# Last image of a state-space, attention and expert-layer kernel: where its first-choice rows are gathered, where its bias is added, and where its residual is kept

## The chip, the cores and the metric

The kernel runs on one core of a Trainium2 chip. Its time is the device time of one execution in microseconds. Shown for the kernel before are three timed runs and one profiled execution; a trace of the profiled execution gives every instruction of every engine. The engines are TensorE (PE, with its weight loads PEld), VectorE (DVE), ScalarE (ACT), GpSimd (POOL) and SyncE, whose queue SP issues nearly all DMAs. All data are fp32.

## The reference, cut to what matters

Four images of 384 channels by 1024 positions pass through three layers. Only the last one, and the sum behind it, is touched here:

```python
# layer 0: four-direction selective scan, normalised, GELU, added to x
# layer 1: t = t + attention(layernorm(t))            # t: (1024 tokens, 384) per image
t = t + ffn(layernorm(t))                             # t on the right is the residual

def ffn(x):                                           # 4 experts, 2 chosen per token
    probs = softmax(x @ gate_w + gate_b)
    masked = probs kept at the two largest, divided by their sum   # the two shares
    h = gelu(einsum("bsd,edh->ebsh", x, w1) + b1[:, None, None, :])      # hidden 1536
    y = einsum("ebsh,ehd->ebsd", h, w2) + b2[:, None, None, :]
    return einsum("bse,ebsd->bsd", masked, y)
```

So the output of one token is its residual, plus share times row of its first expert, plus share times row of its second, where each row has had that expert's bias b2 added.

## The kernel before, in words

The program is written out in "ticks" by generators: each tick lets the scan, the attention, the expert layer and a list of side jobs (`side`) issue a few instructions, and every engine then works through its own instructions in that order. Images 0 to 2 have their attention and expert layer laid beside the scan of the next image. The last image has nothing beside it (`alone`, b = 3), and the end of the program is its expert layer and a closing sum.

**Routing.** `chosen` (L1390) works on groups of 4, 2 and 2 tiles of 128 tokens. It finds the two experts of each token and a place for each of its two rows: expert e owns the rows from e*1024 on of a DRAM array `xs_d`, and the rows of one expert are packed. In `places`, column 0 is the smaller row number, so the first choice is always the lower-numbered of the two experts; column 1 is the second choice. `scatter` (L1513) writes token rows to `xs_d` by 16 indirect DMAs from POOL. The gates (shares by expert) are transposed by PE (L1538), copied by ACT (L1543) and stored to `gates_d` (L1559). `table` (L1565) works out the expert and the block number of each of NBLK = 11 blocks of 256 rows, clipped at L1596 to the 16 blocks that the array has, and how many rows of each block are filled (0, up to 128, up to 256).

**Expert layer.** `experts` (L1622) walks the blocks in the order "1" 0, "1" 1, "2" 0, "1" 2, "2" 1, ... , "1" 10, "2" 9, "2" 10, where "1" is the product with w1 and GELU, "2" the product with w2. PE runs `first_` (L1758) and `second_` (L1808) under branches that skip empty halves of a block; a wholly empty block gets only small fill transposes (L1766, L1817). The weights come in chunks of 384 KB into 8 shared SBUF slots by L1664 on the SP queue. When "2" of block j is done, `out_` (L1824) copies its two halves of 128 rows to the tile `yt`, one half by ACT (L1829), one by DVE (L1827), and `kept` (L1836) stores the tile to the DRAM array `ys_d` (L1837), also on SP. ACT does its copy behind the GELUs of the next block's "1" that stand ahead of it, and what SP holds behind a store (the next chunks of w2) waits for that store.

**Closing sum of the last image.** `kept` of block 2 starts `beside_all` (L1947): for each of the 8 token tiles a load of the residual t2 from DRAM into `z` (L1955; it was stored there by attention at L1266), a load of the gates (L1956), and an ACT scaling of an identity by the second share (L1958). `kept` of block 9 starts `first_choice` (L2021): POOL gathers the first-choice rows of the 8 tiles out of `ys_d` (L1880) and DVE adds share times row to `z` (L1967). `kept` of block 10 starts `late` (L2030): POOL gathers the second-choice rows; PE sums `z` by identity (L1977) and the bias as b2 times gates (L1980) for all 8 tiles, then adds the second choice (L2041), ACT copies the sum (L1913) and SP stores it (L1914).

**What orders these.** A tile is tracked as a whole. A gather from `ys_d` waits for every store to it that stands ahead in the program, and a store to it waits for every gather that stands ahead. A PSUM tile that is two banks wide (`y_end`, `v_end`) is tracked as one, so a reader of one bank can wait for work on the other. [...]

Of the kernel before, what the change touches and what calls it, by code (L numbers as in the profile page):

```python
# [54 lines left out]
CAP = L  # L55
NBLK = 2 * L // BT + E - 1


@with_exitstack
def hybrid_kernel(  # L60
# [146 lines left out]
    gates_d = [dram.tile([E, L], F32, tag=f"gt_{b}", name=f"gtd_{b}") for b in range(B)]  # L207
    xs_d = [dram.tile([E * CAP, C], F32, tag=f"xs_{i}", name=f"xsd_{i}") for i in range(1)]
    ys_d = [dram.tile([E * CAP, C], F32, tag=f"ys_{i}", name=f"ysd_{i}") for i in range(1)]
    views = dram_disjoint_views(xs_d[0], 2 * L // P)  # L210
    g_d = dram.tile([P, M, C], F32, tag="g", name="g_d")
    wv_d = dram.tile([P, M, C], F32, tag="wv", name="wv_d")
# [116 lines left out]
    def later():  # L329
        yield "wait", 8  # L330
        for t, src in (
            (dsk, d_skip), (lnw, ln_w), (lnb, ln_b),
            (gw, gate_w.rearrange("(c p) e -> p c e", p=P)), (gb, gate_b.partition_broadcast(P)),
        ):
            nc.sync.dma_start(t, src)
            yield "wait", 1
        yield "wait", 2
        nc.vector.tensor_reduce(dsum, dsk, AX.X, ALU.add)
        yield "wait", 40
        zero = yield from slots.take("zero", P, C)  # L340
        nc.gpsimd.memset(zero, 0.0)
        yield "wait", 2
        for t in (*xs_d, *ys_d):
            for o in range(0, E * CAP, 8 * P):
                nc.sync.dma_start(
                    t[o : o + 8 * P, :].rearrange("(r p) d -> p r d", p=P),
                    zero.unsqueeze(1).to_broadcast([P, 8, C]),
                )
                yield "wait", 6
        slots.give("zero")  # L350
        for m in range(M):
            nc.sync.dma_start(b2s[:, m * P : (m + 1) * P], b2[:, :, m].rearrange("p e -> e p"))
            yield "wait", 4


# [762 lines left out]
    def attention(b, yb, fx0):  # L1118
# [117 lines left out]
        def values(i):  # L1236
# [14 lines left out]
            def rows():  # L1251
# [17 lines left out]

                if alone:  # L1270
                    kept()
                else:
                    defer(2, kept)
# [116 lines left out]
    def chosen(b, h, sc, rows):  # L1390
# [142 lines left out]
        mts = []  # L1533
        for part in parts:
            pm = yield from banks.take(f"pm_{name}_{part[0]}")
            for q in part:
                o = (q - part[0]) * P
                nc.tensor.transpose(pm[:E, o : o + P], mk[:, q, :], ident)  # L1538
            yield "pe", 0.12 * len(part)
            mt = yield from slots.take(f"mt_{name}_{part[0]}", E, 512)  # L1540
            mts.append(mt)
            yield "wait", 1
            nc.scalar.copy(mt[:, : len(part) * P], pm[:E, : len(part) * P])  # L1543
            banks.give(f"pm_{name}_{part[0]}")
# [20 lines left out]
    def table(b, total):  # L1565
# [29 lines left out]
        nc.vector.tensor_tensor(which[:, 1, :], which[:, 1, :], turn_of[:, :, 0], ALU.add)  # L1595
        nc.vector.tensor_scalar_min(which[:, 1, :], which[:, 1, :], float(E * CAP // BT - 1))  # L1596
        nc.vector.tensor_copy(n, total)
# [24 lines left out]
    def experts(b, route):  # L1622
# [6 lines left out]
        chunks = [(w, j, c) for w, j in order_ for c in range(6)]  # L1629
        tiles, biases = {}, {}  # L1630
        fetched = [0]
        expert, block = {}, {}

        def look_up(j):
            if j == 0:
                expert[j] = block[j] = 0
            if j not in expert:
# [4 lines left out]
                    tables[b][0:1, NBLK + j : NBLK + j + 1], min_val=0,  # L1642
                    max_val=E * CAP // BT - 1,
                )

        def weights():
# [4 lines left out]
            if w == "1":  # L1651
# [140 lines left out]
        def second_(j, gone):  # L1792
# [31 lines left out]
            def out_():  # L1824
                for i in range(2):
                    if alone and i == 1 and j < NBLK - 1:
                        nc.vector.tensor_copy(yt[:, i, :], pss[i][:, :C])  # L1827
                    else:
                        nc.scalar.copy(yt[:, i, :], pss[i][:, :C])  # L1829
                    banks.give(f"py_{b}_{j}_{i}")  # L1830
# [5 lines left out]
            def kept():  # L1836
                nc.sync.dma_start(rows_of(ys_d[0], j), yt)  # L1837
# [39 lines left out]

    def gather(b, i, g, k):

        nc.gpsimd.indirect_dma_start(  # L1880
            out=g[:, k * C : (k + 1) * C], out_offset=None, in_=ys_d[0],
            in_offset=bass.IndirectOffsetOnAxis(ap=places[b][:, i, k : k + 1], axis=0),
        )
# [27 lines left out]
    def put_out(b, i, ps, z):  # L1911

        nc.scalar.copy(z[:, C : 2 * C], ps[:, :C])  # L1913
        nc.sync.dma_start(  # L1914
            out[b, :, i * P : (i + 1) * P].rearrange("(m p) l -> p m l", p=P),
            z[:, C : 2 * C].rearrange("p (m t) -> p m t", m=M),
        )
# [29 lines left out]
    def beside_all(b):  # L1947

        for i in range(L // P):
            g = dtp.tile([P, L], F32, tag=("dt4", "du4")[i // 4], name=f"g_{b}_{i}")  # L1950
            z = (hp if i < 7 else dap).tile(
                [P, L], F32, tag="h" if i < 7 else "da", name=f"z_{b}_{i}"
# [3 lines left out]
            nc.sync.dma_start(g[:E, 2 * C : 2 * C + P], gates_d[b][:, bass.ts(i, P)])  # L1956
            for k in range(2) if b < B - 1 else (1,):
                act(  # L1958
# [4 lines left out]

    def add_choice(b, i, k):

        g, z = closing[b, i]
        nc.vector.scalar_tensor_tensor(  # L1967
            z[:, :C], g[:, k * C : (k + 1) * C], shares[b][:, i, k : k + 1], z[:, :C],
            ALU.mult, ALU.add,
        )  # L1970

    def sum_up(b, i, ps, last):

        g, z = closing[b, i]
        for m in range(M):
            s = bass.ts(m, P)
            nc.tensor.matmul(ps[:, s], z[:, s], ident, start=(m == 0), stop=False)  # L1977
        for m in range(M):
            s = bass.ts(m, P)
            nc.tensor.matmul(  # L1980
                ps[:, s], b2s[:, s], g[:E, 2 * C : 2 * C + P], start=False,
                stop=(last and m == M - 1),
            )
# [36 lines left out]

    def first_choice(b):  # L2021

        for i in range(L // P):
            gather(b, i, closing[b, i][0], 0)
        yield "wait", 2
        for i in range(L // P):
            add_choice(b, i, 0)
            yield "wait", 0

    def late(b):  # L2030
# [4 lines left out]
        for i in range(L // P):  # L2035
            pss[i] = yield from banks.take(f"pz_{b}_{i}")
            sum_up(b, i, pss[i], False)
        for i in range(L // P):
            g, z = closing[b, i]
            for m in range(M):  # L2040
                nc.tensor.matmul(  # L2041
                    pss[i][:, bass.ts(m, P)], g[:, C + m * P : C + (m + 1) * P],
                    z[:, 2 * C + P : 2 * C + 2 * P], start=False, stop=(m == M - 1),
                )
# [181 lines left out]
```

## Time and profile before

| | |
|---|---|
| timed runs | 3621.86, 3630.05, 3631.2 us; median 3630.05 |
| profiled execution | 3634.82 us; span of its trace 3633.1 us; mean granted TensorE clock 0.856 |
| PE busy / DVE busy / ACT / POOL | 80% / 80% / 58% / 55% of the span |
| scan of the four images | first to last scan row, 50.1 to 3054.7 us of the span |
| normalisation, attention and routing of the last image | about 3055 to 3270 us |
| its expert layer | about 3270 to 3588 us |
| its closing sum | about 3588 to 3633 us |
| DMA of the program | 799.22 MB, 220 GB/s on average |

A row of the timeline gives start and length in microseconds, engine, source line, operation, output and inputs, and in brackets how long the engine had been idle and what released it. Matmuls of fp32 show two records each. Instructions that only issue a DMA stand on the queue's own rows (SPq). The clock column of the windows is the granted TensorE clock as a share of full speed. The engines' shares are averages over stages; the last 550 us, in which the scan is over, are read by themselves.

### The profile page before, as it was taken

The numbers are of one execution on the slowest core, as the hardware profiler recorded it, in microseconds if no ns is written. First come the engines' busy times: TensorE is split into PE (matmuls) and PEld (weight loads), VectorE is DVE, ScalarE is ACT, GpSimd is POOL, SyncE is SP. The second block draws the span as 40 slices with busy tenths as digits, with TensorE's granted clock in tenths as the row PEclk, the third lists the DMA queues.
The fourth block names the chain that finished last, engine by engine and source line by source line (L and its number), as shares of the span: only waits on it lengthen the run. The fifth ranks groups of instructions, "written<-read, shape, count | busy, mean of one in ns | idle before, by whom it ended". The sixth has DMA issues, their size and how long they took to land.

```text
span 3633.1 us, 42851 instructions
## 1 busy us (share of the span) xinstructions
PE 2902.2 (80%) x12982; PEld 1682.8 (46%) x12982; DVE 2898.7 (80%) x2148; ACT 2090.0 (58%) x3375; POOL 1982.5 (55%) x950
## 2 busy tenths in 40 slices
PE   4666676778599999679589996678499985889998
PEld 1333333334255664345246562344166651557776
DVE  6998888998999999989998999999999997130000
ACT  4888888557477666458466665457265663332121
POOL 2777677645666566855665556856766666010001
PEclk7777876789699999789689998789599997979997
DMA  6677665554579987644578887644488884125665
GB/s 189 225 257 266 231 220 187 198 171 169 193 250 331 319 307 280 219 176 155 174 251 300 288 309 270 208 161 150 161 297 279 313 309 142 44 75 166 201 198 160
DMA packets 405252, 799.22 MB, mean 220 GB/s; under 512 B 47500, under 2 KB 278620, under 8 KB 404972
## 3 DMA queue, kind: packets, MB, share of 16 engines
q1 hardware_dynamic: 390572, 770.01, 61.3%
q0 software_dynamic: 8192, 25.17, 2.1%
q8 instruction: 165, 2.70, 0.3%
q10 hardware_dynamic: 6208, 0.39, 0.1%
q14 instruction: 115, 0.94, 0.1%
HBM read 680.44 MB, written 115.02 MB: 219 GB/s over the span
## 4 chain that ended last, share of the span: by engine, by line
PE 31%; DVE 27%; DMA 4%; issue 2%; ACT 2%; SPq 0%; POOL 0%; DVEq 0%; ACTq 0%; POOLq 0%
DVE h L716 14%; DVE v L710 9%; PE ph L1758 8%; PE py L1808 7%; PE y L758 2%; DMA w<-in_w 2%; PE v_end L1808 2%; PE y_end L1808 1%; PE pq L1144 1%; PE pv L1155 1%; PE y_end L1758 1%; PE v_end L1758 1%; ACT ht L196 1%; PE ss L1174 0%; PE pdt L566 0%
## 5 line engine op out<-in xcount | busy, mean ns | idle before, releaser
L733 POOL TENSOR_TENSOR h<-h,bc 128x1024 f32<-128x1024 f32 x768 | 1816.8, 2369 | 1101.2 <-DVE v L710 881.3
L716 DVE TENSOR_TENSOR_SCAN h<-da,v 128x1024 f32<-128x1024 f32 x768 | 1749.9, 2284 | 75.6 <-PE v L1032 38.3
L196 ACT ACTIVATE da<-dt,a 128x1024 f32<-128x1024 f32 x768 | 882.5, 1159 | 712.9 <-DVE h L716 587.7
L710 DVE TENSOR_TENSOR v<-du,bc 128x1024 f32<-128x1024 f32 x664 | 863.3, 1300 | 80.3 <-PE y L758 35.4
L758 PE MATMUL y<-h,sel 128*32 128x512 f32 x3072 | 629.3, 719 | 266.6 <-POOL h L733 250.3
L1758 PE MATMUL ph<-turned,w 128*128 128x256 f32 (+1 forms) x2568 | 534.8, 363 | 15.0 <-DMA w<-in_w 9.3
L1808 PE MATMUL py<-w,ht 128*128 128x384 f32 x1416 | 485.9, 493 | 19.0 <-DMA w<-in_w 19.0
L1758 PEld LDWEIGHTS ph<-turned,w 128*128 128x128 f32 x2568 | 449.2, 192 | 105.1 <-issue 17.0
L758 PEld LDWEIGHTS y<-h,sel 128*32 128x32 f32 x3072 | 110.3, 121 | 656.3 <-POOL h L733 416.5
L1808 PEld LDWEIGHTS py<-w,ht 128*128 128x128 f32 x1416 | 265.6, 191 | 233.5 <-issue 46.1
L196 ACT ACTIVATE ht<-ph,b1t 128x256 f32<-128x256 f32 x470 | 195.7, 472 | 238.7 <-PE ph L1758 211.6
L1880 POOL DMA_INDIRECT g<-ysd,places x64 | 85.7, 1338 | 345.8 <-DMA ysd<-yt 329.9
L196 ACT ACTIVATE st<-turn,bt 128x128 f32<-128x128 f32 x832 | 242.6, 543 | 0.0
L1032 PE MATMUL v<-ident,st 128*128 128x128 f32 x832 | 149.1, 339 | 100.0 <-DVE h L716 92.1
L1032 PEld LDWEIGHTS v<-ident,st 128*128 128x128 f32 x832 | 122.3, 176 | 147.1 <-DVE h L716 88.8
L186 ACT ACT_TABLE_LOAD x122 | 156.5, 1283 | 13.2 <-issue 11.0
L566 PE MATMUL pdt<-xd,wdt 12*128 12x512 f32 x184 | 108.9, 739 | 23.8 <-ACT st L196 13.5
L1515 POOL DMA_INDIRECT xsd<-fx,places x32 | 38.7, 1209 | 142.4 <-issue 138.9
L1827 DVE COPY yt<-y_end 128x384 f32<-128x384 f32 x3 | 1.7, 558 | 128.1 <-ACT ht L196 60.1
L1245 PE MATMUL po<-vt,pt 128*128 128x384 f32 x234 | 86.6, 518 | 6.2 <-ACT pt L1135 6.2
L196 ACT ACTIVATE ht<-ht 128x3072 f32<-128x3072 f32 x33 | 91.2, 2765 | 0.4
L1174 PE MATMUL ss<-axn,qt 128*128 128x512 f32 (+3 forms) x240 | 87.1, 503 | 2.8 <-ACT pr L196 1.7
(433 smaller groups left out, 2748.4 us busy)
## 6 DMA issues: line engine op xcount, KB each, us to landing
w<-in_w SPq DMA_DIRECT2D x528, 384.0 KB
bc<-rows SPq DMA_DIRECT2D x384, 512.0 KB
dt<-dts SPq DMA_DIRECT2D x192, 512.0 KB
du<-dts SPq DMA_DIRECT2D x192, 512.0 KB
dts<-dt SPq DMA_DIRECT2D x48, 512.0 KB
dts<-du SPq DMA_DIRECT2D x48, 512.0 KB
xg<-xsd SPq DMA_DIRECT2D x44, 384.0 KB
ysd<-yt SPq DMA_DIRECT2D x44, 384.0 KB
```

The lines of the kernel that those rows point to most:

```text
L186: nc.scalar.preload_act_table_set(kind)
L196: return nc.scalar.activation(dst, src, f, **more)
L566: nc.tensor.matmul(pss[i], wdt[r, m * P : (m + 1) * P], xd[r, bass.ts(h, 512)], start=True, stop=True,)
L710: return nc.vector.tensor_tensor(u["v"], spread["du4", n], spread["bc", n][:, 0, :], ALU.mult)
L716: nc.vector.tensor_tensor_scan(u["h"][:, ::step], u["da"][:, ::step], u["v"][:, ::step], 0.0, op0=ALU.mult, op1=ALU.add,)
L733: product = units[n]["product"] = nc.gpsimd.tensor_tensor(h, h, spread["bc", n][:, 1, :], ALU.mult)
L758: units[n]["row"] = nc.tensor.matmul(y, sel, h, start=first, stop=last, tile_position=(0, jj * DJ))
L1032: nc.tensor.transpose(u["v"][:, t * P : (t + 1) * P], st[:, t, u["j"] * P : (u["j"] + 1) * P], ident)
L1174: nc.tensor.matmul(ps[:, : e - o], qt[:, c, i * P : (i + 1) * P], xn[o // 512][:, c, : e - o], start=(c == 0), stop=(c == M - 1 and (alone ...
L1245: nc.tensor.matmul(po[:, :C], pts[i][:, j, :], vt[:, j, :], start=False, stop=(j == i))
L1758: nc.tensor.matmul(ps[:, i * BT : i * BT + n], t[:, c, i * P : (i + 1) * P], xt[:, c, :n], start=(c == 0), stop=(c == M - 1),)
L1808: nc.tensor.matmul(pss[i][:, :C], hts[j][:, 2 * c + f, i * P : (i + 1) * P], tiles["2", j, c][0][:, f, :], start=(c == 0 and f == 0), stop ...
```

## The change

1. `ys_d` and `xs_d` grow from 4096 to ROWS = 4864 rows, so that empty surplus blocks get rows of their own, and the clip in `table` goes. The zero fill of both at the start (`later`) grows from 8 to 10 DMAs. `ys_d` gets two views that are declared disjoint: `up_to_last` and `the_last`. In the last image, blocks 0 to 9 are stored through the first, block 10 through the second.
2. First choices are gathered through `up_to_last`, at one of two places, by branches that POOL takes. Behind block 8, if block 9 belongs to the last expert (no first choice is of the last expert, so all their rows are then stored); else behind block 9. The additions of share times row stand behind block 9 as before.
3. b2 is also written to DRAM once (`b2_d`); for each block of the last image its expert's row is loaded to all 128 partitions (`b2t`), on SP's queue ahead of the block's first w2 chunk. Both halves of `yt` are made by DVE as PSUM plus `b2t`; ACT makes none.
4. The residual stays in SBUF (`yb`): its stores, its loads, the gates' transposes, copies, stores and loads of the last image go; DVE adds the first choice into `yb`; the closing PE sum is `yb` by identity and the second choice, without the bias product; `late` uses the gather tile for its copy.

On the engines' order up to the routing of the last image, only SP's rows change (more zero fill, the write of `b2_d`, later b2 loads), and three clips on DVE go. In DVE's order at the end stand: two additions of block 9, eight first-choice additions, two additions of block 10.

```diff
+ROWS = E * CAP + (NBLK - 2 * L // BT) * BT
-    ys_d = [dram.tile([E * CAP, C], F32, tag=f"ys_{i}", name=f"ysd_{i}") for i in range(1)]
+    ys_d = [dram.tile([ROWS, C], F32, tag=f"ys_{i}", name=f"ysd_{i}") for i in range(1)]
+    b2_d = dram.tile([E, C], F32, tag="b2", name="b2_d")
+    up_to_last, the_last = dram_disjoint_views(ys_d[0], 2)
...
-            for o in range(0, E * CAP, 8 * P):
+            for o in range(0, ROWS, 8 * P):
+                n = min(8, (ROWS - o) // P)
...
+        nc.sync.dma_start(b2_d, b2s)
...
-                if alone:
-                    kept()
-                else:
+                if not alone:
                     defer(2, kept)
...
-        for part in parts:
+        for part in () if alone else parts:
...
+                if alone and c == 0:
+                    b2ts[j] = bcp.tile([P, 2, L], F32, tag="bc", name=f"b2t_{b}_{j}")[:, 0, :C]
+                    row_ = b2_d[bass.ds(e, 1), :]
+                    nc.sync.dma_start(
+                        b2ts[j], bass.AP(
+                            tensor=row_.tensor, offset=row_.offset, ap=[[0, P], row_.ap[-1]]
+                        )
+                    )
...
-                    if alone and i == 1 and j < NBLK - 1:
-                        nc.vector.tensor_copy(yt[:, i, :], pss[i][:, :C])
+                    if alone:
+                        nc.vector.tensor_tensor(yt[:, i, :], pss[i][:, :C], b2ts[j], ALU.add)
...
-                nc.sync.dma_start(rows_of(ys_d[0], j), yt)
+                there = (up_to_last if j < NBLK - 1 else the_last) if alone else ys_d[0]
+                nc.sync.dma_start(rows_of(there, j), yt)
...
+                elif alone and j == NBLK - 3:
+                    side.append(first_choice(b, True))
                 elif alone and j == NBLK - 2:
                     side.append(first_choice(b))
...
     def beside_all(b):
...
+            if b == B - 1:
+                closing[b, i] = g, g[:, :C]
+                act(g[:, 2 * C : 2 * C + P], ident, AF.Copy, scale=shares[b][:, i, 1:2])
+                yield "wait", 1
+                continue
...
+    def add_choice(b, i):
+
+        g, _ = closing[b, i]
+        t2 = ybs[b][:, :, bass.ts(i, P)]
         nc.vector.scalar_tensor_tensor(
-            z[:, :C], g[:, k * C : (k + 1) * C], shares[b][:, i, k : k + 1], z[:, :C],
+            t2, g[:, :C].rearrange("p (m t) -> p m t", m=M), shares[b][:, i, 0:1], t2,
             ALU.mult, ALU.add,
         )
...
-    def first_choice(b):
+    ahead_of = {}
 
-        for i in range(L // P):
-            gather(b, i, closing[b, i][0], 0)
+    def first_choice(b, soon=False):
+
+        def gathers():
+            for i in range(L // P):
+                gather(b, i, closing[b, i][0], 0, up_to_last)
+
+        if soon:
+            ahead_of[b] = nc.gpsimd.value_load(
+                tables[b][0:1, NBLK - 2 : NBLK - 1], min_val=0, max_val=E - 1
+            )
+            with tc.If(ahead_of[b] > E - 2):
+                gathers()
+            return
+        with tc.If(ahead_of[b] < E - 1):
+            gathers()
         yield "wait", 2
         for i in range(L // P):
-            add_choice(b, i, 0)
+            add_choice(b, i)
             yield "wait", 0
```

More of the change, by code (lines that the diff above doesn't have):

```diff
@@ L207, in hybrid_kernel @@
     gates_d = [dram.tile([E, L], F32, tag=f"gt_{b}", name=f"gtd_{b}") for b in range(B)]
-    xs_d = [dram.tile([E * CAP, C], F32, tag=f"xs_{i}", name=f"xsd_{i}") for i in range(1)]
-    ys_d = [dram.tile([E * CAP, C], F32, tag=f"ys_{i}", name=f"ysd_{i}") for i in range(1)]
+    xs_d = [dram.tile([ROWS, C], F32, tag=f"xs_{i}", name=f"xsd_{i}") for i in range(1)]
+    ys_d = [dram.tile([ROWS, C], F32, tag=f"ys_{i}", name=f"ysd_{i}") for i in range(1)]
     views = dram_disjoint_views(xs_d[0], 2 * L // P)
+    b2_d = dram.tile([E, C], F32, tag="b2", name="b2_d")
+    up_to_last, the_last = dram_disjoint_views(ys_d[0], 2)
     g_d = dram.tile([P, M, C], F32, tag="g", name="g_d")
@@ L343, in later @@
         for t in (*xs_d, *ys_d):
-            for o in range(0, E * CAP, 8 * P):
+            for o in range(0, ROWS, 8 * P):
+                n = min(8, (ROWS - o) // P)
                 nc.sync.dma_start(
-                    t[o : o + 8 * P, :].rearrange("(r p) d -> p r d", p=P),
-                    zero.unsqueeze(1).to_broadcast([P, 8, C]),
+                    t[o : o + n * P, :].rearrange("(r p) d -> p r d", p=P),
+                    zero.unsqueeze(1).to_broadcast([P, n, C]),
                 )
@@ L1595, in table @@
         nc.vector.tensor_tensor(which[:, 1, :], which[:, 1, :], turn_of[:, :, 0], ALU.add)
-        nc.vector.tensor_scalar_min(which[:, 1, :], which[:, 1, :], float(E * CAP // BT - 1))
         nc.vector.tensor_copy(n, total)
@@ L1629, in experts @@
         chunks = [(w, j, c) for w, j in order_ for c in range(6)]
-        tiles, biases = {}, {}
+        tiles, biases, b2ts = {}, {}, {}
         fetched = [0]
@@ L1642, in look_up @@
                     tables[b][0:1, NBLK + j : NBLK + j + 1], min_val=0,
-                    max_val=E * CAP // BT - 1,
+                    max_val=ROWS // BT - 1,
                 )
@@ L1876, in experts, with gather @@
                 yield from second_(j, gone[j])
-    def gather(b, i, g, k):
+    def gather(b, i, g, k, there=None):
         nc.gpsimd.indirect_dma_start(
-            out=g[:, k * C : (k + 1) * C], out_offset=None, in_=ys_d[0],
+            out=g[:, k * C : (k + 1) * C], out_offset=None,
+            in_=ys_d[0] if there is None else there,
             in_offset=bass.IndirectOffsetOnAxis(ap=places[b][:, i, k : k + 1], axis=0),
@@ L1911, in put_out @@
     def put_out(b, i, ps, z):
-        nc.scalar.copy(z[:, C : 2 * C], ps[:, :C])
+        at_ = z if b == B - 1 else z[:, C : 2 * C]
+        nc.scalar.copy(at_, ps[:, :C])
         nc.sync.dma_start(
             out[b, :, i * P : (i + 1) * P].rearrange("(m p) l -> p m l", p=P),
-            z[:, C : 2 * C].rearrange("p (m t) -> p m t", m=M),
+            at_.rearrange("p (m t) -> p m t", m=M),
         )
@@ L1956, in beside_all @@
             nc.sync.dma_start(g[:E, 2 * C : 2 * C + P], gates_d[b][:, bass.ts(i, P)])
-            for k in range(2) if b < B - 1 else (1,):
+            for k in range(2):
                 act(
@@ L1962, in beside_all, with sum_up @@
             yield "wait", 1
-    def add_choice(b, i, k):
-        g, z = closing[b, i]
+    def add_choice(b, i):
+        g, _ = closing[b, i]
+        t2 = ybs[b][:, :, bass.ts(i, P)]
         nc.vector.scalar_tensor_tensor(
-            z[:, :C], g[:, k * C : (k + 1) * C], shares[b][:, i, k : k + 1], z[:, :C],
+            t2, g[:, :C].rearrange("p (m t) -> p m t", m=M), shares[b][:, i, 0:1], t2,
             ALU.mult, ALU.add,
         )
-    def sum_up(b, i, ps, last):
-        g, z = closing[b, i]
+    def sum_up(b, i, ps):
         for m in range(M):
[L1976 to L1979, printed above, removed]
             nc.tensor.matmul(
-                ps[:, s], b2s[:, s], g[:E, 2 * C : 2 * C + P], start=False,
-                stop=(last and m == M - 1),
+                ps[:, bass.ts(m, P)], ybs[b][:, m, bass.ts(i, P)], ident, start=(m == 0),
+                stop=False,
             )
@@ L2036, in late @@
             pss[i] = yield from banks.take(f"pz_{b}_{i}")
-            sum_up(b, i, pss[i], False)
+            sum_up(b, i, pss[i])
         for i in range(L // P):
@@ L2042, in late @@
                     pss[i][:, bass.ts(m, P)], g[:, C + m * P : C + (m + 1) * P],
-                    z[:, 2 * C + P : 2 * C + 2 * P], start=False, stop=(m == M - 1),
+                    g[:, 2 * C : 2 * C + P], start=False, stop=(m == M - 1),
                 )
```

## The prediction

> **What bounds the kernel now.** The change leaves the engines' order of the first 3190 us or so as it was, so I read the end. First the windows of equal stages, for where PE still fills its time:
>
> ```profile
> 3510.00:3545.00 35.00, 34.43 (x155) 27.72 (x154) 1.11 (x2) 10.76 (x27) 0.00 (x0) 1.00 0.68 224
> 3545.00:3569.00 24.00, 19.10 (x76) 11.96 (x74) 0.56 (x1) 6.18 (x17) 0.00 (x0) 0.96 0.53 168
> 3569.00:3587.00 18.00, 18.00 (x48) 10.26 (x49) 0.00 (x0) 0.00 (x0) 0.00 (x0) 0.86 0.61 198
> 3587.00:3595.00 8.00, 0.86 (x7) 0.58 (x5) 0.76 (x2) 1.34 (x3) 1.10 (x2) 0.76 0.43 129
> 3595.00:3621.00 26.00, 25.47 (x97) 21.88 (x98) 4.80 (x8) 0.00 (x0) 14.09 (x15) 0.50 0.44 130
> 3621.00:3633.00 12.00, 7.80 (x48) 7.42 (x48) 0.00 (x0) 3.82 (x8) 0.00 (x0) 0.78 0.46 131
> ```
>
> After the stage come its length, then busy time of PE, PEld, DVE, ACT and POOL, the clock, the DMA share and GB/s. Up to 3587 the expert layer is bound by PE; the last 46 us are the closing sum. The timeline there, in order:
>
> ```profile
> 3587.24 0.48 ACT L1829 COPY yt<-v_end 128x384 f32<-128x384 f32 x1 [20.47 <-PE py L1808]
> 3587.24 0.56 DVE L1827 COPY yt<-py 128x384 f32<-128x384 f32 x1 [25.70 <-PE py L1808]
> 3587.93 18.51 SPq L1837 DMA_DIRECT2D ysd<-yt  x2
> ...
> 3591.69 0.98 POOL L1880 DMA_INDIRECT g<-ysd,places  x1 [323.84 <-DMA ysd<-yt]
> 3594.80 0.68 DVE L1967 SCALAR_TENSOR_TENSOR z<-g,shares,z 128x384 f32<-128x384 f32 x1 [6.99 <-DMA g<-ysd,places]
> ...
> 3609.46 0.94 POOL L1880 DMA_INDIRECT g<-ysd,places  x1 [6.11 <-DMA ysd<-yt]
> ...
> 3618.21 0.95 POOL L1880 DMA_INDIRECT g<-ysd,places  x1 [0.30 <-issue]
> ...
> 3620.75 2.93 PE L2041 MATMUL pz<-z,g 128*128 128x128 f32 x12
> ...
> 3629.41 0.48 ACT L1913 COPY z<-y_end 128x384 f32<-128x384 f32 x1 [1.02 <-PE y_end L2041]
> ```
>
> Two stores stand in one SP row of 18.51 us: block 9's at 3587.93, and block 10's at 3606.0 (the stores' own rows say so). SP's list of waits names why:
>
> ```profile
> SPq L1837 <- DMA g<-ysd,places: 1.2, 1, 1.2
> ```
>
> Block 10's store waits for the first-choice gathers, since they read the array that it writes, and the second-choice gathers wait for block 10's store. So two trains of gathers stand in series, 3591.69 to 3603.36 and 3609.46 to 3619.16. PE is busy 25.47 of 26 us meanwhile, at half clock: 16 steps of 1.57 us, residual and bias for eight tiles. Both end near 3621, so removing either alone gains nothing.
>
> Last, where PE waits inside the expert layer:
>
> ```profile
> 3391.80 1.65 SPq L1664 DMA_DIRECT2D w<-in_w  x3
> 3395.46 0.88 PE L1808 MATMUL y_end<-w,ht 128*128 128x384 f32 x2 [2.74 <-DMA w<-in_w]
> ...
> 3564.60 0.40 SPq L1837 DMA_DIRECT2D ysd<-yt  x1
> 3568.91 1.62 PE L1808 MATMUL v_end<-w,ht 128*128 128x384 f32 x2 [4.54 <-DMA w<-in_w]
> ```
>
> The other two such waits are 1.38 (at 3335.61) and 0.67 (at 3488.26). In each, chunks of w2 stand in SP's queue behind something late.
>
> **Which way the branch goes.** Block 10 shows only fill transposes (L1766 from 3560.5), so it is empty. Then block 9 is the last filled one or an empty one, and in either case has the last expert: the gathers go behind block 8.
>
> **The new end, step by step, in the time of this trace.** PE ends block 9 at 3587.2.
> - Block 9's two additions, now both on DVE: PSUM and SBUF in, 128x384. The PSUM copy of this size took 0.56, the SBUF addition at L1967 0.625; I take 0.6 each. They end at 3588.4 (before: 3587.8, two engines side by side).
> - Eight additions of first choices, in DVE's order next: 8 x 0.625 = 5.0, to 3593.4. Their data are there: block 8's store leaves at about 3564, its gathers start 3.76 later (3587.93 to 3591.69), take 11.7 (as the first train did) and land 2.1 after (3592.67 to 3594.80): 3581.7, slack 6.7 us.
> - Block 10's two additions are queued behind these: 1.2, to 3594.6; store at 3594.8. Its own view takes away the wait for gathers.
> - Store to first second-choice gather: 3.76 and 3.46 in the two cases here; 3.6, so 3598.4.
> - One train of eight: 9.7 (the second train), or 11.7 as the first, which had one gap of 2.2. I take 9.7: end 3608.1, landed 3610.2.
> - PE's residual sum is eight steps of 1.57, following DVE from 3589.1: done by 3602, no longer late. The last three matmuls and the copy take what they took: 3628.44 to 3633.1 = 4.7. End 3614.9.
>
> That is 18.2 less than 3633.1. Late next is the chain DVE, store, gathers, not PE.
>
> **Upstream.**
> - Residual and gate loads go. Sixteen of them stood in SP at 3385.1 to 3394.8, ahead of and among the chunks for the matmul at 3395.46. In full blocks without them chunks follow the store at once (3361.0, then 3361.69) and land 3.5 later; here they would land near 3389.5, and PE needs them at 3392.7. Gain 2.74, and the clock drop behind that wait, 1.9 (pairs of 0.88, 0.88, 1.28, 1.28, 0.83 against 0.65): 4.6, bounds 0 and 4.6.
> - ACT's copy of `yt` goes, so two stores no longer wait behind its GELUs. In the changed order the additions at the two short blocks (3324, 3477) read single-bank tiles and wait for PE alone, so the stores can leave some 5 us sooner: 1.38 + 0.67 = 2.0 gained, bounds 0 and 2.0. At block 8 one half still waits for ACT through the two-bank `y_end`: store about 0.5 sooner, nothing more.
> - The bias row: one more DMA of 192 KB per block ahead of the w2 chunks, 0.65 of SP's queue each (store to chunk, 3564.60 to 3565.23). Full blocks have 2.6 to 4 us between landing and need, which hides it; without that cover it costs 0.65 a block, 7 in all. At block 9 it is seen: +0.65 - 0.5 = +0.15.
> - The early gathers move 8 x 192 KB each way of the memory, about 1.6 MB, while block 9's chunks load at 198 GB/s. Over 18 us that is 87 GB/s more, 285 in sum; 365 GB/s was moved in a 20 us window at 360 to 380. I take +0.5, between 0 (chunks after the second are not needed until 3574 and later) and 4.3 (1.6 MB at 365, all of it in the way).
> - Gates' path and residual stores in routing: ACT copies of 0.57 and 0.36 and two PE transposes (0.44, 0.58) stand in the chain of 3215 to 3238. Gain 1.0, between 0 and 1.5; the third group's wait for them (7.2 us at 3268) is hidden behind the load of `xg`, 4.0 more.
> - Zero fill: two more DMAs, 2.36 MB, and the write of b2, near 400 to 450. DVE was busy 90% of 200 to 240 without such DMAs and 89% of 240 to 380 with eight. +0.5, between 0 and 3 (two DMA waits of 1.6 at most there). Three clips of 0.16 on DVE go: nothing.
>
> [...] POOL now branches. [...] The nearest rows: PE's branches around empty halves show "issue" gaps of 0.2 to 0.3 us, and one gap of 2.2 us on POOL has no other named cause. [...]
>
> **Sum.** -18.2 - 4.6 - 2.0 - 1.0 + 0.15 + 0.5 + 0.5 = -24.7. Against the profiled execution's 3634.8 this gives 3610.1, and against the median of the runs, 4.8 below it, 3605.
>
> **Rivals.**
> - *Main case, 3605, chance 0.52.* Both trains apart, most stalls gone: 3600 to 3610.
> - *SP's queue takes the upstream gain back, 3612, chance 0.22.* Two additions one after another (+0.6) and the bias row (+0.65) hold the chunks, so the waits at the short blocks stay or grow. For: every PE wait in the layer ends at `w`. Against: the order lets those additions start earlier. -24.7 + 6.6 = -18, median 3612.
> - *The end is shorter still, 3598, chance 0.10.* Additions nearer 0.56 (1.0 less), the wait of 4.5 at block 9 going down with ACT relieved (4.5 less, with clock).
> - *The early branch isn't taken, or its path is late: 3618, chance 0.10.* Then the first train starts at 3592.3, the additions end at 3606.8, and block 10's additions stand behind them: store at 3608.1, the second train 3611.6 to 3621.3, end 3628.1. That is -5.0, with -6.5 upstream about -12. Against it: block 10 is empty.
> - *Slower, 3650, chance 0.06.* DVE alone makes `yt`, and where it reads a two-bank PSUM tile it waits for ACT's GELU of the other bank. If that moves each store of a block by more than the 2.6 us which chunks have in hand, PE stalls at each of nine boundaries as at block 9: 4.5 and a clock drop of 1.9, 58 us less the 24.7 and the waits replaced, some 20 to 33. Against: ACT's copy stood behind all six GELUs too, so the store moves by 0.8 at most.
>
> The range takes in the second, third and nearly the fourth case: 3596 to 3619. A measurement of this kernel can tell 0.3%, 11 us, from no change. Faster by that (below 3619) 0.87, within 0.07, slower 0.06.
>
> **What would show it.** Right: POOL's first train near 3568 to 3580 of this clock, well before block 9's "2" ends; block 10's store within 7 us of block 9's, with no wait for gathers; eight steps of residual sum in PE's rows instead of sixteen, none with b2; PE's wait on `w` only at block 9. Wrong: a POOL or DVE gap behind the branch; PE waits on `w` at full blocks; `b2t` rows in SP's waits; or the first 3190 us longer than here by more than 3.

## The result, and the profile after

| | before | after |
|---|---|---|
| timed runs | 3621.86 to 3633.92 us (8), median 3628.05 | 3607.32 to 3620.48 us (8), median 3613.24 |
| profiled execution; span | 3634.82; 3633.1 us | 3612.04; 3610.3 us |
| mean granted clock | 0.856 | 0.859 |

The ratio is 0.9961, with a 95% interval of 0.9948 to 0.9974: faster by 14.8 us between the medians, and by 22.8 between the two profiled executions. The forecast was 3605, with a range of 3596 to 3619, and a gain of 24.7. So sign and range held, while some 60% of the gain came; the main case's own stretch, 3600 to 3610, did not hold.

The end, from the timeline of the changed kernel (columns as before):

```profile
3580.87 0.56 DVE L1837 TENSOR_TENSOR yt<-v_end,b2t 128x384 f32<-128x384 f32 x1 [26.30 <-DMA w<-in_w]
3581.34 0.55 DVE L1837 TENSOR_TENSOR yt<-y_end,b2t 128x384 f32<-128x384 f32 x1
3581.81 4.31 DVE L1988 SCALAR_TENSOR_TENSOR yb<-g,shares,yb 128x384 f32<-128x384 f32 x8
3581.92 5.55 SPq L1848 DMA_DIRECT2D ysd<-yt  x2
...
3586.04 1.02 DVE L1837 TENSOR_TENSOR yt<-py,b2t 128x384 f32<-128x384 f32 x2
...
3590.35 0.94 POOL L1893 DMA_INDIRECT g<-ysd,places  x1 [20.05 <-DMA ysd<-yt]
...
3599.09 0.95 POOL L1893 DMA_INDIRECT g<-ysd,places  x1 [0.30 <-issue]
...
3601.49 1.65 PE L2070 MATMUL v_end<-g 128*128 128x128 f32 x6 [1.33 <-issue]
...
3606.44 0.48 ACT L1928 COPY g<-pz 128x384 f32<-128x384 f32 x1 [0.22 <-PE pz L2070]
```

This is the order that was forecast: block 9's two additions, eight of first choices, block 10's two, its store 5.2 us after block 9's (both stand in the SP row of 5.55), then one train of gathers instead of two. The row of 18.51 us is gone. New is the stretch behind the last gather: it is issued by 3600.04, yet the last copy starts at 3606.44. At 3601.49 the fifth tile's product starts 0.05 us after ACT's copy of the fourth, which lies in the same two-bank tile `v_end`, and runs at half clock (1.65 for six records). The granted clock of that stretch (the sixth number behind the length, counts in brackets left out), and of the same stretch in `bias_behind`, a kernel described below that has the same instructions there:

```profile
3601.40:3604.00 2.60, 2.51 (x11) 2.51 (x12) 0.00 (x0) 0.52 (x2) 0.00 (x0) 0.50 0.49 156
...
3590.40:3592.70 2.30, 1.62 (x12) 1.43 (x13) 0.00 (x0) 0.48 (x1) 0.98 (x2) 1.00 1.02 290
```

At 0.50 the stretch from the end of the last gather's issue to the end of the kernel took 10.2 us, at 1.00 it took 8.2.

Where PE waited in the expert layer (PE's waits from 3255 to 3582: total us, times, longest):

```profile
PE y_end L1707 <- DMA xg<-xsd: 11.9, 1, 11.9
PE v_end L1818 <- DMA w<-in_w: 7.2, 1, 7.2
PE v_end L1707 <- ACT ht L197: 1.5, 1, 1.5
PE y_end L1707 <- ACT ht L197: 1.3, 2, 0.9
PE v_end L1818 <- ACT ht L197: 1.2, 1, 1.2
PE v_end L1827 <- ACT ht L197: 0.9, 1, 0.9
```

The three waits for `w` at blocks 1, 3 and 6 (1.38, 2.74, 0.67) are gone. In the places of two of them, at blocks 3 and 6, stand waits for ACT's GELUs (0.3 and 1.2), and the one at block 9 has grown from 4.5 to 7.2. Its timeline:

```profile
3554.02 0.56 DVE L1837 TENSOR_TENSOR yt<-y_end,b2t 128x384 f32<-128x384 f32 x1 [1.97 <-ACT ht L197]
...
3554.60 0.40 SPq L1848 DMA_DIRECT2D ysd<-yt  x1
3555.20 1.25 SPq L1666 DMA_DIRECT2D b2t<-b_d  x1
...
3556.68 3.60 SPq L1674 DMA_DIRECT2D w<-in_w  x6
...
3562.08 1.62 PE L1818 MATMUL v_end<-w,ht 128*128 128x384 f32 x2 [7.21 <-DMA w<-in_w]
```

From block 8's store to the start of block 9's "2" it took 4.3 us before (3564.60 to 3568.91) and takes 7.5 now. The bias row holds SP for 1.25 us, not 0.65, and the chunk lands 5.3 after its issue instead of 3.6.

The span cut at landmarks that both kernels have, in us. In brackets are the values of kernels made later in which that stretch is the changed kernel's:

| stretch | before | after | forecast | found |
|---|---|---|---|---|
| start to the last scan instruction | 3052.4 | 3046.7 (3038.5 to 3055.0) | +0.5 | within spread |
| to the first scatter of the last image | 157.5 | 157.2 | 0 | -0.3 |
| to the first transpose of `xg` | 63.1 | 59.7 (57.2 to 62.2) | -1.0 | -3.4 |
| expert layer, to the end of block 9's "2" | 314.2 | 317.1 (315.2 to 317.2) | -5.95 | +2.9 |
| from there to the end | 45.9 | 29.5 (27.5 to 29.5) | -18.2 | -16.4 |

The 5.7 us of the first row are no work of the change that I can show: with the same instructions up to there, the last scan instruction of eleven later kernels starts anywhere from 3038.5 to 3049.4, of a twelfth at 3055.0. Without it the profile's gain is 17.1, near what the medians say. The stage that failed is the expert layer.

### The profile page after: what moved, and what is told of

The parts are those of the page before. It is cut to its first block, busy times and chain, and to the rows that moved or that the text cites. A ratio compares the mean times of both kernels' runs of the same rounds, so it can differ in the third digit from the quotient of the medians.

```text
span 3610.3 us, 42761 instructions
## 1 busy us (share of the span) xinstructions
PE 2877.7 (80%) x12926; PEld 1662.9 (46%) x12926; DVE 2904.0 (80%) x2156; ACT 2086.1 (58%) x3360; POOL 1982.4 (55%) x950
## 5 line engine op out<-in xcount | busy, mean ns | idle before, releaser
L1818 PE MATMUL py<-w,ht 128*128 128x384 f32 x1536 | 525.5, 492 | 20.3 <-DMA w<-in_w 20.3
L1768 PE MATMUL ph<-turned,w 128*128 128x256 f32 (+1 forms) x2532 | 526.9, 363 | 13.6 <-DMA w<-in_w 6.8
L1818 PEld LDWEIGHTS py<-w,ht 128*128 128x128 f32 x1536 | 288.0, 191 | 248.5 <-issue 40.4
```

Of the source, the lines that this page charges most:

```text
L1768: nc.tensor.matmul(ps[:, i * BT : i * BT + n], t[:, c, i * P : (i + 1) * P], xt[:, c, :n], start=(c == 0), stop=(c == M - 1),)
L1818: nc.tensor.matmul(pss[i][:, :C], hts[j][:, 2 * c + f, i * P : (i + 1) * P], tiles["2", j, c][0][:, f, :], start=(c == 0 and f == 0), stop ...
```

## The experiments

Theory: the end gains by the early train alone; in the layer the loads' removal gains what was forecast, and waits for ACT and the chunk at block 9 take it back. Rivals: the disjoint view parts the trains; branches on POOL cost microseconds; the layer's loss is the bias row, or the early gathers, or the order of banks. Kernels of one group ran beside the same runs of the kernel before; "changed kernel" is the one of `as_is`, or of the first result.

**Which half of the end counts.** Kernel `no_view`:

```diff
-    there = (up_to_last if j < NBLK - 1 else the_last) if alone else ys_d[0]
+    there = up_to_last if alone else ys_d[0]
```

> The changed kernel, but the last block's rows are stored through the same view of the array as all others, so that its store must again wait for the gathers of first choices. Theory A (the early gathers, behind block 8, are what parts the two trains, and they are done near 3573, long before that store is issued near 3587): from the end of block 9's last matmul to the end of the span 29.5 us as in the changed kernel, within 1; total within 3 of it. Theory B (the own view is what parts the trains): the store waits and that stretch grows by 10 or more.

Measured: 3601.95 us, ratio 0.9954 (0.9938 to 0.9969); block 9 to the end 29.3. So the view alone is worth nothing once the early train is there: that train's last issue was at 3561.9, 15 us ahead of the store that would have to wait.

`late_train` takes the branch and the early call away:

```diff
-            ahead_of[b] = nc.gpsimd.value_load(
-                tables[b][0:1, NBLK - 2 : NBLK - 1], min_val=0, max_val=E - 1
-            )
-            with tc.If(ahead_of[b] > E - 2):
-                gathers()
             return
-        with tc.If(ahead_of[b] < E - 1):
-            gathers()
+        gathers()
```

> The changed kernel without the branch of GpSimd: the first choices are always gathered behind block 9, as in the kernel before; the own view, the bias at the copy and the residual on chip stay. Theory A: block 10's additions stand on VectorE behind the eight additions of first choices, so the own view alone helps little: from block 9's end, store 1.1, first gather 4.7, a train of 10 to 12, the last landing and addition by 18, block 10's store 19.5, its train from 23 to 33, and 8 to 10 behind the last issue: 42 to 43 instead of 29.5, so 11 to 13 slower than the changed kernel. Theory B (the own view parts the trains by itself): 0 to 4 slower. On the start of block 9's second matmul: if the early gathers delay its first chunk, the time from block 8's store to its start falls from 7.5 to about 5.5 here; if the bias row does, it stays at 7.

Measured: 3617.36, ratio 1.0001 (0.9991 to 1.0011); block 9 to the end 41.7. In its timeline DVE holds back the store:

```profile
3569.14 20.08 SPq L1848 DMA_DIRECT2D ysd<-yt  x2
3573.06 0.98 POOL L1893 DMA_INDIRECT g<-ysd,places  x1 [325.41 <-DMA ysd<-yt]
...
3587.78 1.01 DVE L1837 TENSOR_TENSOR yt<-py,b2t 128x384 f32<-128x384 f32 x2
3592.05 0.94 POOL L1893 DMA_INDIRECT g<-ysd,places  x1 [6.94 <-DMA ysd<-yt]
```

Block 10's additions run at 3587.78, behind the first choices, so the two stores are 20 us apart again, though the view lets the store pass. The whole change without the early train shows no gain in the total. By the stretches it should keep some 5 us, 4.2 of them at the end; the interval allows 3.3, and that difference stays unexplained. The start of block 9's "2", 7.3 after block 8's store, shows that the early gathers are not what delays it.

**The price of a branch on POOL.** `no_branch` issues the early gathers with no branch, which holds for these inputs only:

```diff
-            ahead_of[b] = nc.gpsimd.value_load(
-                tables[b][0:1, NBLK - 2 : NBLK - 1], min_val=0, max_val=E - 1
-            )
-            with tc.If(ahead_of[b] > E - 2):
-                gathers()
+            gathers()
             return
-        with tc.If(ahead_of[b] < E - 1):
-            gathers()
```

> The changed kernel with the gathers behind block 8 issued with no branch (this holds for these inputs, where block 9 belongs to the last expert). If branches on GpSimd cost under 1 us each and pass while it waits: the first early gather 3.9 to 4.1 us after block 8's store as in the changed kernel (3554.60 to 3558.64), the first second-choice gather 3.3 behind block 10's store, total within 2. If each of them stalls for some 2 us: the first early gather about 2 us sooner after its store, or the second train 2 sooner.

Measured: 3602.29, ratio 0.995 (0.9931 to 0.997). First early gather 4.12 after block 8's store (3.6 to 4.2 in the kernels with branches), second train 3.26 after block 10's store (3.27 in the changed kernel). So no cost of the branches shows within a spread of 0.6 us. The gap of 2.2 us behind the first gather, which the prediction could not name, is there without branches too (2.21), so the branches don't make it.

**The bias row.** `bias_behind`:

```diff
-                if alone and c == 0:
+                if alone and c == 3:
```

> The changed kernel with the bias row of each block loaded ahead of the fourth chunk of its w2 instead of the first. Theory A (the row holds up the first chunk at block 9, by its 1.25 us in the queue of SyncE and by its 192 KB): from block 8's store to the start of block 9's second matmul 5.0 to 5.8 instead of 7.5, total 1.5 to 2.5 faster. Theory B (the early gathers delay the chunk): 6.5 to 7, total 0.5 faster. In the other blocks nothing, as no wait for a chunk is left there.

Measured: 3601.67, ratio 0.9955 (0.9937 to 0.9972). Block 9:

```profile
3549.03 0.40 SPq L1848 DMA_DIRECT2D ysd<-yt  x1
3549.67 2.24 SPq L1674 DMA_DIRECT2D w<-in_w  x3
...
3554.30 1.62 PE L1818 MATMUL v_end<-w,ht 128*128 128x384 f32 x2 [5.09 <-DMA w<-in_w]
```

5.3 from store to product instead of 6.9 to 7.6: some 2 us of the 3.2 lost there are the row's. The early gathers still run beside, so what the other 1 us is stays open. It isn't the row's time in SP's queue alone: in `rotate` (below) the row holds SP for 0.34 us and the chunk is issued 1.2 after the store, not 2.1, yet the product starts 7.4 after it. The layer took 314.2, 1 to 3 less than in the changed kernel; the total can't tell 2 us.

**The spread.** `as_is` is the changed kernel once more.

> The changed kernel once more, unaltered, beside the kernels of this group on one chip. Its ratio to the kernel before again 0.995 to 0.9975. If the 5.7 us by which its scan ended sooner in the first profile belonged to the change, the scan's last instruction starts at 3046 to 3047 again; if it was the spread between runs, it moves by some us.

Measured: 3605.57 (3595.48 to 3606.68), ratio 0.9956 (0.9942 to 0.9969). Its scan's last instruction starts at 3047.3, as foreseen; but other kernels with the same scan lie up to 9 away, so this settles nothing on the 5.7 us. Its layer took 315.2, its end 28.9.

**The removed loads.** `loads_back` puts sixteen loads back; they read image 0's rows and gates, which nothing uses:

```diff
                 act(g[:, 2 * C : 2 * C + P], ident, AF.Copy, scale=shares[b][:, i, 1:2])
+                z = (hp if i < 7 else dap).tile(
+                    [P, L], F32, tag="h" if i < 7 else "da", name=f"z_{b}_{i}"
+                )
+                nc.sync.dma_start(z[:, :C], t2_d[0][bass.ts(i, P), :])
+                nc.sync.dma_start(z[:E, 2 * C : 2 * C + P], gates_d[0][:, bass.ts(i, P)])
```

> The changed kernel with sixteen loads put back behind block 2's store, of the kernel before's sizes (residual rows and gates of another image, into tiles that nothing reads). Theory A (these loads held back the chunks for block 3's second matmul, 2.74 and a clock drop of 1.6 to 1.9): the wait for a chunk there comes back with 2 to 4 us, the total is 3 to 5 above the changed kernel. Theory B (waits for ACT's GELUs that came in their place are the next bound, and take up part of it): 1 to 2 above. Theory C (the loads had a free place in the queue): 0.

Measured: 3607.54, ratio 0.9968 (0.9955 to 0.9982), 2.0 by medians and 4.3 by the ratios above `as_is`. The wait at block 3 came back:

```profile
PE py L1818 <- DMA w<-in_w: 3.3, 1, 3.3
```

The stretch around it, from the first product behind block 5's transposes (they stand in the middle of block 4's "1") to the first behind block 3's "2", took 28.5 instead of 23.9: 4.6, the forecast's own number. The total alone could not show it, as the two intervals overlap.

**The routing, and what came with it.** `routing_back` puts the gates' path and the residual's stores back, unused:

```diff
+                if alone:
+                    kept()
...
-        for part in () if alone else parts:
+        for part in parts:
```

> The changed kernel with the gates' path (transposes, copies, stores) and the residual's stores put back into the last image's routing; nothing reads them. Theory A (they stood in the chain between the scatters of the three groups: 25.98 us between the first two groups' scatters before, 22.84 after): 25.5 to 26 again there, the load of xg 2.5 to 3 later; against that, PE's transposes break its 11.9 us of idle time ahead of the expert layer, so less time at half clock follows: total 1 to 2.5 above the changed kernel. Theory B (the 3.1 came from elsewhere): 22 to 24 between the scatters, total within 1.

Measured: 3612.98, ratio 0.998 (0.9971 to 0.999). The first two groups' scatters are 26.5 apart (26.0 before, 22.3 to 23.6 in the changed kernel and the ten others without the path) and the first transpose of `xg` comes 63.8 after the first scatter, as before. But the layer took 321.7, which I had not expected: waits for chunks are back.

```profile
PE v_end L1820 <- DMA w<-in_w: 12.4, 3, 8.0
...
PE y_end L1778 <- DVE yt L1839: 3.6, 2, 1.8
```

The code hands the eight PSUM banks around in turn. Three takes for the gates' transposes, one for each group of tiles, had gone, so every later product had come into another bank. `rotate` gives those takes back, with a one-element fill in place of the work:

```diff
+        for part in parts if alone else ():
+            spun = f"pm_{name}_{part[0]}"
+            nc.vector.memset((yield from banks.take(spun))[:1, :1], 0.0)
+            yield "pe", 0.12 * len(part)
+            yield "wait", 1
+            banks.give(spun)
```

> The changed kernel, in whose last routing a PSUM bank is still taken and given back at each place where the gates' path took one, with nothing of that path computed but a one-element fill of the bank. This gives every later product of the last expert layer the bank that it has in the kernel before. Theory A (the change also moved the rotation of banks: block 0's and block 5's second products went from the two-bank tiles to banks of their own, and no longer wait there for ACT's GELUs): waits of PE for chunks return at block ends as where the gates' path was put back (12.4 us on chunks in all, of which 7 to 8 at block 9), and the stretch from the first transpose of xg to block 9's first addition grows by 3 to 5 us, the total by 2 to 5. Theory B (the bank order is of no account, and putting the gates' path back costs by its chain alone): total within 1 of the changed kernel.

Measured: 3613.86, ratio 0.9978 (0.9966 to 0.999), as slow as with the whole path back; layer 325.3; first two groups' scatters 25.4 apart, first scatter to `xg` 62.5.

```profile
PE v_end L1824 <- DMA w<-in_w: 14.2, 3, 8.3
```

Its stores of blocks 0 and 5 leave 7.3 us after PE's last product (1.1 in the changed kernel, 6.5 before), since DVE again reads halves of `v_end` and `y_end` and waits for GELUs of their other halves. Block 0's additions, in `rotate` (PE's last product ends at 3318.82), and in the changed kernel (3316.60):

```profile
3325.02 0.56 DVE L1843 TENSOR_TENSOR yt<-v_end,b2t 128x384 f32<-128x384 f32 x1 [61.60 <-ACT ht L197]
3325.50 0.55 DVE L1843 TENSOR_TENSOR yt<-y_end,b2t 128x384 f32<-128x384 f32 x1
...
3316.64 1.02 DVE L1837 TENSOR_TENSOR yt<-py,b2t 128x384 f32<-128x384 f32 x2 [56.81 <-PE py L1818]
```

So most of what taking out the gates' path was worth, some 3 us in the routing and 5 to 10 in the layer, came from the places that it gave up in the order of the banks, not from its work. The run also gives back the path's ticks; what these did apart from the banks was not tried.

**The new chain.** `store_first` moves the eight additions from `first_choice` to behind the gathers in `late`, so block 10's two additions go first:

```diff
         yield "wait", 2
-        for i in range(L // P):
-            add_choice(b, i)
-            yield "wait", 0
...
         for i in range(L // P):
+            add_choice(b, i)
             pss[i] = yield from banks.take(f"pz_{b}_{i}")
```

> The changed kernel with VectorE's order turned at the end: block 10's two additions and its store go ahead of the eight additions of first choices. Theory A (after the change the end is bound by DVE, store, gathers in series): the eight additions, 4.3 us, leave the path, and the stretch from block 9's first addition to the end falls from 29.4 to 25 or 26, the total by 3.5 to 4.3. Theory B (the second train waits for something else, such as block 9's store or PE's sums): 0 to 1.

Measured: 3601.04, ratio 0.9947 (0.9934 to 0.9961), 4.5 by medians below `as_is`, 3.3 by ratios, which the intervals do not part; block 9 to the end 25.8 against 28.9 (27.5 at the least without this edit). The second train starts 5.5 us after block 9's first addition instead of 9.5, so the end was bound by DVE, store, gathers.

`tight_end` adds `bias_behind` and the tiles' order, so that both products of the shared two-bank tile are issued ahead of their copies:

```diff
-        for i in range(L // P):
+        for pair in ((0,), (1,), (2,), (3, 4), (5,), (6,), (7,)):
+            for i in pair:
...
-            put_out(b, i, pss[i], z)
+            for i in pair:
+                put_out(b, i, pss[i], closing[b, i][1])
```

> The changed kernel with three edits: block 10's store ahead of the eight additions, the bias row loaded ahead of the fourth chunk, and the last products of the fourth and fifth tile, which lie in one two-bank tile, both issued ahead of their copies. From the runs of each of the first two: block 9's start 1.5 to 2 us sooner, the stretch from block 9's first addition to the end 25.7; the third, if the wait for ACT's copy at the fifth tile and its half clock are what makes the last copy late, takes 1 to 3 more: 23 to 25. Total 5 to 8 below the changed kernel, 1.3% less uncertain than that: 0.993 to 0.9945 of the kernel before. If the second train then waits for block 9's store or PE's sums, the stretch stays at 25.7.

Measured: 3596.02, ratio 0.9932 (0.9918 to 0.9945); layer 314.2; block 9 to the end 24.1.

```profile
3569.96 1.01 DVE L1837 TENSOR_TENSOR yt<-py,b2t 128x384 f32<-128x384 f32 x2
3570.07 1.32 SPq L1848 DMA_DIRECT2D ysd<-yt  x2
3570.89 4.31 DVE L1988 SCALAR_TENSOR_TENSOR yb<-g,shares,yb 128x384 f32<-128x384 f32 x8
...
3574.61 1.42 POOL L1893 DMA_INDIRECT g<-ysd,places  x1 [13.64 <-DMA ysd<-yt]
```

The two stores now stand in one row of 1.32, and the train starts 5.6 after block 9's first addition instead of 9.5. Of the 4.9 that the end became shorter than in `as_is`, 3.2 came with the store's edit. The other 1.7 can't be given to the pair's order: behind the last gather this kernel took 8.2, but so did `bias_behind`, without that edit, and `warm` took 8.4, where the clock had risen to 1.00 for the last tiles as it had here. This kernel has the lowest ratio of the study, though its interval overlaps those of `store_first` and `own_banks`.

**Half clock.** `warm` has twelve transposes of the identity in each of the two long waits:

```diff
+                if alone and j == 0 and m0 == 0:
+                    for k in range(12):
+                        nc.tensor.transpose(ps[:, (k % 4) * P : (k % 4 + 1) * P], ident, ident)
...
+                    if alone and j == NBLK - 2:
+                        for k in range(12):
+                            nc.tensor.transpose(pss[0][:, (k % 3) * P : (k % 3 + 1) * P], ident, ident)
```

> The changed kernel with twelve transposes of the identity on PE ahead of the first block's transposes (in its wait for xg), and twelve more ahead of block 9's second product (in its wait for the first chunk); their results are overwritten. Theory A (half clock after these waits costs time: 36 products in 10.6 instead of 7.9 us at the layer's start, and the products from 3562 to 3568 at 1.6 and 1.5 a pair instead of 0.8 at block 9): the first stretch (first transpose of xg to the next block's) falls from 11.6 to 12.7 down to 9.5 to 10.5, block 9's second product from its start to its first addition from 17 to 19 down to 15.5 to 16.5, total 2 to 5 less. Theory B (the chunks, not the clock, set the pace of block 9's first products): the second stretch stays.

Measured: 3604.23, ratio 0.9952 (0.9937 to 0.9967), no change that can be told. The first stretch stayed at 12.5: its 36 products took 11.1. At block 9 the product took 17.3 instead of 18.5 or 18.7, but started no sooner; and it took 17.2 in `no_view` and `late_train` too, without transposes, so this isn't their work.

**Block 8's banks.** `own_banks` is `tight_end` with two single banks for block 8:

```diff
+                        if alone and j == NBLK - 3:
+                            banks.free.sort(key=lambda f: (f[0] > clock[0], f[1] >= BANKS))
                         pss[i] = yield from banks.take(f"py_{b}_{j}_{i}")
```

> The kernel with the three edits at the end (block 10's store first, bias row ahead of the fourth chunk, fourth and fifth tile's products ahead of their copies), in which block 8's second product also takes two single-bank tiles instead of one and half of a two-bank one. Theory A (block 8's store waits 2 us for ACT's GELU of the other half, and block 9's chunks stand behind it): the store leaves 1.1 to 1.3 us after block 8's last product instead of 3.1, block 9's second product starts 6 us after it instead of 8.2, and nothing else moves: 1.5 to 2.2 below the kernel with three edits, so 0.992 to 0.9935 of the kernel before. Theory B (the chunks wait for something else, such as free slots): the start stays at 8.

Measured: 3607.34, ratio 0.9941 (0.9927 to 0.9954), no gain over `tight_end`. The store left 1.1 after the last product instead of 3.1, as expected, and block 9's "2" began after 7.2 instead of 8.2: half of it came. PE's fills now wait 1.8 for ACT, the closing sums lie in other banks, and at the very end one gather landed late (a wait of 3.2), so block 9 to the end took 27.0.

## Why the prediction was right, and where its sizes were off

- **The end, -18.2: right, 1.8 too much.** The steps up to the train were each a little shorter: two additions 1.0 (1.2 forecast), eight 4.2 (5.0), two 0.9 (1.2), store to gather 3.3 (3.6 and 0.2 to the store). The train was 9.7 as said. Landing and last work, "the last three matmuls and the copy take what they took", were taken at 6.8 and took 10.2: that step failed. It carried over the end of a kernel in which the last products came late and in one run (0.78 granted on average); now they follow the gathers one by one, at 0.50. What the runs show of it is the clock: of seven kernels with the same instructions there, five had 0.50 for the sixth and seventh tile, and this stretch took 9.6 to 10.2; two had 1.00 (`bias_behind`, `warm`), and it took 8.2 and 8.4. What the pair's order in the shared tile costs apart from that was not shown.
- **"Late next is the chain DVE, store, gathers, not PE": right**, shown by `store_first`.
- **"Removing either alone gains nothing" was said of trains and residual sum: not borne out at the end.** `late_train` leaves the trains in series and takes the bias half of PE's sum away; its last train ends 1.8 us later than before, yet block 9 to the end is 4.2 shorter (41.7 against 45.9), since only 8.0 us instead of 13.9 follow the train. In the total nothing of it shows. The own view was counted as what frees block 10's store; `no_view` shows that the early train alone does.
- **Residual and gate loads, -4.6: right**, by `loads_back`.
- **Two stores no longer behind GELUs, -2.0: mechanism right, gain absent.** The stores do leave 5.4 us sooner (1.1 after the last product, not 6.5) and the waits for chunks went. But between block 0's and block 1's "2" PE needs 11.6 us before and after, and between block 5's and 6's 10.9 and 12.3: ACT's GELUs of a short block are due at nearly the same time, and PE now waits for them. The prediction named what was late there, and did not ask what was second. That the stores do leave sooner was luck in part: it hangs on the change of banks, which the prediction read from the order of instructions without weighing it, and with the old banks (`rotate`) the layer is 8 to 10 us longer.
- **Waits for ACT that no step had, +2.3** between blocks 1 and 2 (18.7 us from the last product of one to the first of the other's "2", 16.4 before; two waits of 0.93 stand in it). With the old banks (`rotate`) it is 16.4 again.
- **Half clock at the layer's start, +1.85** from the first transpose of `xg` to the next block's (0.8 in `as_is`). PE starts there at 0.50 before and after, but the clock rises later (before, 0.50 for the first 4.1 us, then 0.97 for 3.0; now 0.50 for 4.4, then 0.61 for 4.0): the first 36 products take 10.6 instead of 9.2; the rest is a wait for ACT's copy ahead of them, 0.7 instead of 0.25. The gates' transposes stood in PE's wait for `xg`, which is now 11.9 us in one piece; that this is the cause is not shown, and `rotate` speaks against it, since PE idles 11.8 in one piece there and the 36 take 9.3.
- **Bias row and early gathers at block 9, +0.65: mis-sized.** The wait measured +2.7 and the product +0.4. The row was sized by its 0.65 us of SP's queue; it held SP for 1.25, and the chunk behind it took 1.7 longer to land. `bias_behind` gives 2 of it to the row, `late_train` next to nothing to the gathers, and 1 stays open. By these terms the layer lost 2.0 + 2.3 + 1.85 + 2.45 = 8.6 of the 8.85 between forecast and measurement.
- **Routing, -1.0: right in sign, -3 in size** (63.1 against a mean of 60.2 in eleven kernels without the path). `rotate` shows that most of it was not the removed work.
- **Branches on POOL, for which the sum has no term: right**: `no_branch` shows no cost of them within 0.6.

Of the rivals, the second came nearest: what SP and ACT take back upstream is about 9 us, and its time, 3612, is 1 us from the median. But its mechanism, that waits for chunks at the short blocks stay, is not what happened.

That the range held rests on the end. Upstream, from the first scatter to block 9, 6.95 us were forecast to go and 0.5 did, and the 3 us of the routing that are in this came mostly from an effect that the prediction had not seen.

## What to carry to other kernels

A wait that goes uncovers the next one: ask for each place what was second latest there, and by how much, before the gain is booked. Taking out work that took its turn at a shared resource also moves every later user to another place in the rotation; compare who shares with whom before and after. And when a long wait at the end goes, look again at the work behind it, its order and the clock it is granted, which nobody could see while it was hidden.

## What the runs showed of the hardware that was not expected

**Twelve transposes in the wait for `xg` did not end the half clock behind it.** From `warm`: the granted clock in the twelve transposes, in the pause behind them, and in the first products.

```profile
3253.60:3256.50 2.90, 2.81 (x12) 2.42 (x12) 1.34 (x7) 0.00 (x0) 0.64 (x1) 0.50 0.35 127
3256.50:3260.00 3.50, 0.89 (x7) 0.64 (x6) 0.00 (x0) 0.13 (x1) 0.00 (x0) 0.99 0.52 139
3260.50:3264.00 3.50, 3.49 (x8) 2.86 (x9) 0.00 (x0) 1.51 (x2) 0.00 (x0) 0.50 1.03 345
```

2.9 us of transposes ran at 0.50, the clock rose to 0.99 in the 3.5 us behind them, of which PE was busy for 0.89, and fell to 0.50 in the first 3.5 us of the products. In the changed kernel, which has no such transposes, it was 0.50 for the 4.4 us behind the wait, 0.61 for the next 4.0 and 1.00 for the 8 behind those. What sets the clock in these stretches was not shown.

**The first gather of a first train left a gap of 2.2 us** before the second in eleven kernels, with branches or without, after pauses of POOL of 298 to 325 us; in their second trains, after pauses of 6 to 20 us, that gap was 0.30. What makes the gap was not tried.

**The same stretch differs between groups of runs.** From the last scan instruction to the first scatter took 157.2 to 157.5 us in the three profiles taken where the kernel before ran at medians of 3626 to 3628 us, and 149.1 to 151.1 in all eleven others, at 3619 to 3621. What in it is slower was not looked into.
